# Slots of a batch ordered by key half, then head pair, with three key halves and one set of value chunks on chip, in a paged attention kernel

## The chip, the cores and the metric

One core of one Trainium2 chip. The time is the device time of one launch in microseconds; the profile is one further execution of the same program with the hardware profiler on.

## What is computed

64 sequences of 32 tokens, 512 features. First each sequence is mixed over its own tokens with one of 16 weight matrices, and added to itself:

```python
x = x + jnp.einsum('bct,bcd->bdt', x, weights[condition])     # 32 x 32 each
```

Then a layer of attention with a paged cache is added. 32 query heads share 8 key heads of 128; q and k are normed and rotated; every sequence sees up to 474 of 512 cached keys (16 pages of 32, found by a block table) and its own 32 new ones:

```python
q = rope(rmsnorm(x @ Wq.T));  k = rope(rmsnorm(x @ Wk.T));  v = x @ Wv.T
kc = k_cache[block_table].reshape(bsz, 512, 8, 128);  vc = v_cache[block_table]...
valid_c = arange(512)[None, :] < cache_seqlens[:, None]
scores = jnp.where(valid, q . concat([kc, k]) * SCALE, -1e30)
o = softmax(scores) . concat([vc, v]);   x = x + o @ Wo.T
```

## The kernel before, in words

All is fp32. The work is cut into 32 **steps**: two halves of the heads (16 query heads, 4 key heads each), and in each 16 token tiles of 128 rows. A tile is 4 sequences, called **batches** (`bt`). A step has 16 **slots**, four for each batch; a slot is numbered `g` inside its batch and `slot` inside the step. The loop over steps, batches and slots (in the part behind L1380 of the listing) calls the pieces below in the order that is written there, and the scheduler is told to keep that order on every engine, so the program order is the order of each engine's queue.

A slot deals with two of the four key heads (a pair: heads 0 and 1, or 2 and 3) against half of the 512 cached keys (256, two chunks of 128). `part_of(j)` names pair and half of slot `j`: before the change, pair 0 half 0, pair 0 half 1, pair 2 half 0, pair 2 half 1. In a slot there are:

- `scores` (L859): four products (eight rows of the profile, two passes each) of keys by queries into the PSUM tile `ps`, then `exp` on ScalarE (L870) into `pr`, of which there are two buffers. No maximum is subtracted.
- `head_keys` (L850): DVE copies the keys of the slot four ahead from `k_t` into `kh` (four buffers).
- `load_half` (issues at L324): SyncE (SP) loads half a batch of keys, eight pages, for the batch two ahead, into `k_t` (four halves). It is called at `g` = 0 and 1.
- `next_values`: ScalarE fills one chunk of `v_ring` (L370) from `raw`, multiplying by `valid`, which is 1 for keys that the sequence has and 0 for others. `v_ring` holds two batches of four chunks, each with a further column that holds `valid` itself, written on GpSimd (L373, `mask_ones`), so that the product with values also gives the sum of the softmax. Behind each fill GpSimd issues the indirect fetch of the chunk three further on (L357) into the freed `raw` (three buffers).
- `values` (L922) of the slot before: four products of `pr` by `v_ring` into the PSUM tile `po` (two buffers), which collects both halves of a pair. In the first four slots of a step they stand early in the slot, in the others at its end. After the second half of a pair, DVE adds `nv` (what the new keys gave), takes the reciprocal and multiplies (L933 to L936): "the triple".

Beside this, a step carries pieces of the steps around it: `new_scores` at slot 0 and `new_values` at slots 1 and 2 (L880, L904, with copies of `nv` on ScalarE, L912) for the new keys; `turn` (L946) of finished outputs on DVE at slots 0, 10 and 13; the output projection `out_proj` (L787) of the step before; and a `plan` of pieces that project later tiles to q, k and v. Two tiles are projected together with seven half-sized products in place of eight (L691, PSUM banks `pa`, `pb`, `pc`, sums in `u`, `z` on DVE, L707). The projections are squared on ScalarE (L474), turned into a power on GpSimd (L482, L483), rotated and scaled on DVE (L491 to L509), transposed into `rows` (L534), written to DRAM by GpSimd (L538, `heads_d`) and read back in column order by SP (L546, `spread`) into `q_ring`. `pp` names four PSUM banks that these pieces share.

Before the loop an opening, written out by hand, computes the first tiles (L1060 to L1180).

At the end of the program the softmax's sums are looked at (`in_range`); if one were out of range, the whole would run again in an exact form (`run(True)`).

Of the kernel before, what the change touches and what calls it, by code (L numbers as in the profile page):

```python
# [12 lines left out]
F32 = mybir.dt.float32  # L13
# [7 lines left out]
P = 128  # L21
# [39 lines left out]
def cond_resid_paged_attention_kernel(  # L61
# [55 lines left out]
    part = const.tile([P, 1], F32, tag="part", name="part")  # L117
    nc.vector.tensor_copy(part, part_i)

    valid = const.tile([P, B, VC], F32, tag="valid", name="valid")  # L120
# [46 lines left out]
    def cached_rows(pages_at, lens_at):  # L167

        row2 = const.tile([P, 1], F32, tag="row2", name="row2")
        nc.vector.tensor_scalar(row2, row, float(NHH), None, ALU.mult)  # L170
        nc.vector.tensor_scalar(
            v_row, pages_at, float(PSIZE * NHH), row2, ALU.mult, ALU.add
        )
        nc.vector.tensor_copy(lens_all, lens_at)
        for c in range(VC):
            key = const.tile([P, 1], F32, tag=f"key{c}", name=f"key{c}")
            nc.vector.tensor_scalar_add(key, part, float(c * P))
            nc.vector.tensor_scalar(valid[:, :, c], lens_all, key, None, ALU.is_gt)

    def other_half(by):  # L180

# [21 lines left out]
    def steps_of(exact, pools):  # L203
# [15 lines left out]
        else:  # L219
# [5 lines left out]


        v_ring = wpool.tile(
            [P, 2 * VC, GH, D + 1], F32, tag="v_ring", name=f"v_ring_{uid}"
        )

        def v_of(b):
            return v_ring[:, b % 2 * VC : (b % 2 + 1) * VC]

        vn_bufs = [
            wpool.tile([P, GH, D + 1], F32, tag=f"vn{i}", name=f"vn{i}_{uid}")
# [79 lines left out]
        def load_k(hh, b, half):  # L315

            if half == 0:
                pages_of[hh, b] = page_numbers(b)
            page = pages_of[hh, b]
            k_raw = kv.tile(  # L320
                [P, HP, GH, PSIZE], F32, tag="k_t", name=f"k_t_{hh}_{b}_{half}_{uid}", bufs=4
            )
            for j in range(HP):
                nc.sync.dma_start(  # L324
                    k_raw[:, j, :, :].rearrange("p g r -> p (g r)"),
                    kt[hh, bass.ds(page[half * HP + j], 1)].rearrange("o d e -> (o d) e"),
                )
            return k_raw

        def load_all(hh, b):  # L330
            k_raw = kv.tile([P, NPP, GH, PSIZE], F32, tag="k_all", name=f"k_t_{hh}_{b}_{uid}")
            page = page_numbers(b)
            for j in range(NPP):
                nc.sync.dma_start(
                    k_raw[:, j, :, :].rearrange("p g r -> p (g r)"),
                    kt[hh, bass.ds(page[j], 1)].rearrange("o d e -> (o d) e"),
                )
                r, c = j % BT * PSIZE, j // BT
                ins = nc.sync.dma_start(
                    v_of(b)[r : r + PSIZE, c, :, 0:D],  # L340
                    vc.rearrange("(p r h) (g d) -> p h r g d", r=PSIZE, h=NHH, g=GH)[
                        bass.ds(page[j], 1), hh
                    ].rearrange("o r g d -> (o r) g d"),
                )
                last_k[:] = [ins.ins]
            return k_raw
# [17 lines left out]
            )  # L364
            raws[n, c] = raw

        def mask_v(b, c, raw):

            ok = valid[:, b, c : c + 1]
            nc.scalar.activation(v_of(b)[:, c, :, 0:D], raw, AF.Copy, scale=ok)  # L370

        def mask_ones(b):
            nc.gpsimd.tensor_copy(  # L373
                v_of(b)[:, :, :, D], valid[:, b, :].unsqueeze(2).to_broadcast([P, VC, GH])
            )


        class Step:
# [433 lines left out]
        class Batch:  # L812


            def __init__(self, st, bt):
                self.st, self.bt = st, bt
                self.n = st.n * BT + bt
                self.name = f"{st.name}_{bt}"
                self.b = st.t * BT + bt
                self.k_raw, self.k, self.pr = [], {}, {}  # L820
                if exact:
                    self.k_raw = load_all(st.hh, self.b)
                self.v_t = v_of(self.b)

            def load_half(self):
                self.k_raw.append(load_k(self.st.hh, self.b, len(self.k_raw)))

            def fill(self, c):
                mask_v(self.b, c, raws.pop((self.n, c)))
                if c == 0:  # L830
                    mask_ones(self.b)

        def part_of(j):
            return j // 2 * 2, j % 2

        def queries(ba, g):
            return columns(ba.st, ba.bt)[:, g, :]
# [14 lines left out]

        def scores(ba, j):

            g, _ = part_of(j)
            ps = ps_s.tile([P, 2, 2, P], F32, tag="ps", name=f"ps_{ba.name}_{j}")
            for c in range(2):
                for i in range(2):
                    nc.tensor.matmul(  # L859
                        ps[:, c, i, :],  # L860
                        ba.k[j][:, i, c, :],
                        queries(ba, g + i),
                        start=True,
                        stop=True,
                    )
# [4 lines left out]
            nc.scalar.activation(pr, ps, AF.Exp, scale=SCALE)  # L870
            ba.pr[j] = pr

        def new_scores(st):
# [40 lines left out]
        def values(ba, j):  # L914


            g, half = part_of(j)
            if half == 0:
                ba.po = ps_o.tile([P, 2, D + 1], F32, tag="po", name=f"po_{ba.name}_{j}")
            for c in range(2):  # L920
                for i in range(2):
                    nc.tensor.matmul(  # L922
                        ba.po[:, i, :],
                        ba.pr[j][:, c, i, :],
                        ba.v_t[:, 2 * half + c, g + i, :],
                        start=(half == 0 and c == 0 and i == 0),
                        stop=(half == 1 and c == 1),
                        skip_group_check=True,
                    )
            if half:  # L930
                both = slice(g, g + 2)
                t = ba.st.nv[:, ba.bt, both, :]
                nc.vector.tensor_tensor(t, ba.po, t, ALU.add)  # L933
# [131 lines left out]
        spare["kh", 0, GH - 1], spare["pr", 0, 2] = early[:, 0:512], early[:, 512:1024]  # L1065
# [25 lines left out]
        load_w("q", 0, 3)  # L1091
        later = Batch(first, 1)
        later.load_half()
        later.load_half()
# [7 lines left out]
        rot_tables(first)  # L1102
        nc.vector.memset(vn_bufs[0][:, :, D : D + 1], 1.0)
        nc.vector.memset(vn_bufs[1][:, :, D : D + 1], 1.0)
        cached_rows(pages_at, lens_at)
        trig = work.tile([P, 3, TRIG * HD], F32, tag="w1", name="trig1", bufs=1)
        reduced(TRIG, trig)
# [12 lines left out]
        fetch(0, RAW, tag="pn", bufs=1)  # L1120
        q_b(first, 0)
        head_keys(batch, 0, nc.scalar)
        head_keys(batch, 1, nc.scalar)
        q_a(first, 2)
        k_b(first)
        head_keys(batch, 2, nc.scalar)
# [4 lines left out]
        after.load_half()  # L1131
        after.load_half()
        new = v_product(first)
        q_b(first, 1)
# [6 lines left out]
        batch.fill(2)  # L1141
        fetch(1, 2)
        batch.fill(3)
        scores(batch, 1)
        values(batch, 0)
        q_a(first, 3)
        q_b(first, 2)
# [1 line left out]
        keep_x1(second, nc.gpsimd)  # L1149
        head_keys(later, 0, nc.scalar)  # L1150
        head_keys(later, 1, nc.scalar)
        rot_tables(second)
        k_a(second)
        q_b(first, 3)
        scores(batch, 2)
        scores(batch, 3)
        new_scores(first)
        scores(later, 0)
        new_values(first, 0)
        values(batch, 1)  # L1160
        values(batch, 2)
        new_values(first, 2)
        for c in range(VC):
            later.fill(c)
            fetch(1 + (c + RAW) // VC, (c + RAW) % VC)
        head_keys(later, 2)
# [152 lines left out]
        valued, turned = (batch, GH - 1), [batch]  # L1319
        new_ot(first)  # L1320
        batches = {0: batch, 1: later, 2: after}
        unfilled = [(n, c) for n in range(2, NHH * NT * BT) for c in range(VC)]

        def batch_of(n):
            if n not in batches:
# [34 lines left out]
        for st in steps:  # L1360
            for bt in range(0 if st.n else 1, BT):
# [3 lines left out]
                for g in range(GH):  # L1365
# [3 lines left out]
                    while copied <= min(this.n * GH + g + KH, NHH * NT * BT * GH - 1):  # L1369
                        head_keys(batches[copied // GH], copied % GH)  # L1370
                        copied += 1
                    if g < 2 and this.n + 2 < NHH * NT * BT:
                        batch_of(this.n + 2).load_half()
                    if slot in norm_slots[min(st.n, 4 + st.n % 2)]:
                        norm_next()
# [125 lines left out]
```

## Time and profile before

| what | value |
|---|---|
| median of 3 runs | 2113.44 us (2112.53 to 2113.55) |
| the profiled execution | 2118.78 us |
| its span | 2116.8 us |
| mean granted TensorE clock | 0.994 |
| PE busy | 2082.0 us, 98% |
| DVE, ScalarE, GpSimd busy | 67%, 45%, 48% |
| DMA | 413.22 MB, 195 GB/s |

A page of the profile lists busy times by engine (PE is TensorE's matmuls, PEld its weight loads, DVE VectorE, ACT ScalarE, POOL GpSimd, SP SyncE), and then groups of instructions: the line, the engine, what is written and read, the number, busy microseconds and mean nanoseconds of one, and last how long the engine was idle just before them and what ended that. "A <- B" in a wait means that A waited for B. PEclk is the clock that TensorE was granted, 1.00 being full speed. The profiled execution is 5.3 us longer than the median of the runs; about 2 us of it lie outside the span.

### The profile page before, as it was taken

How to read it: one execution, taken by the hardware profiler on the slowest of the kernel's cores; microseconds unless marked ns; L12 is line 12 of the kernel's file. 1: busy time of each engine (PE TensorE's matmuls, PEld its weight loads, DVE VectorE, ACT ScalarE, POOL GpSimd, SP SyncE). 2: the span in 40 equal slices, each digit the busy share in tenths (PEclk: the TensorE clock that was granted, in tenths of full speed). 3: DMA queues.
4: the chain of work that ended last, by engine and by line, in shares of the span. 5: the costliest groups of instructions: out<-in, count | busy, mean ns of one | idle time of the engine just before them, and what ended most of it. 6: DMA issues, size and time to landing. Idle time of an engine off the chain costs nothing.

```text
span 2116.8 us, 43551 instructions
## 1 busy us (share of the span) xinstructions
PE 2082.0 (98%) x12804; PEld 1469.1 (69%) x12804; DVE 1423.9 (67%) x2930; ACT 960.3 (45%) x2706; POOL 1019.1 (48%) x1250
## 2 busy tenths in 40 slices
PE   7999999999999999999999999999999999999998
PEld 4766666776677766777676677767777776777775
DVE  4555676867768677686866768677676866758532
ACT  3544344544544544444444445434444444445442
POOL 4444365554636456363554535445363554535431
PEclk9999999999999999999999999999999999999999
DMA  8776547576676766787667876666766666675662
GB/s 247 196 204 203 163 133 227 165 212 185 195 215 180 215 183 189 216 253 227 198 204 208 235 213 175 206 183 186 205 192 197 179 198 182 199 205 171 194 202 69
DMA packets 410247, 413.22 MB, mean 195 GB/s; under 512 B 58928, under 2 KB 325552, under 8 KB 410000
## 3 DMA queue, kind: packets, MB, share of 16 engines
q1 hardware_dynamic: 354096, 229.87, 38.3%
q0 software_dynamic: 55168, 180.27, 28.5%
q8 instruction: 104, 1.70, 0.3%
q14 instruction: 143, 1.17, 0.2%
q10 hardware_dynamic: 736, 0.21, 0.0%
HBM read 350.09 MB, written 60.03 MB: 194 GB/s over the span
## 4 chain that ended last, share of the span: by engine, by line
PE 88%; DMA 3%; DVE 2%; SPq 2%; issue 1%; POOL 1%; ACT 1%; ACTq 0%; DVEq 0%; POOLq 0%
PE po_x L922 20%; PE pout_x L787 20%; PE ps_x L859 20%; PE pb_x L691 9%; PE pa_x L691 6%; PE pc_x L691 6%; PE pnv_x L904 2%; PE pp_q_x L465 2%; DMA k_t_x<-in_kt_dram 1%; PE psn_x L880 1%; SPq L324 1%; DMA wo_x<-in_wo_dram 1%; DMA freq<-in_inv_freq_dram 1%; POOL raw_x L357 1%; PE pp_k_x L465 0%
## 5 line engine op out<-in xcount | busy, mean ns | idle before, releaser
L357 POOL DMA_INDIRECT raw_x<-in_vc_dram,v_row x512 | 553.8, 1082 | 497.5 <-ACT v_ring_x L370 403.0
L870 ACT ACTIVATE pr_x<-ps_x 128x512 f32<-128x512 f32 x511 | 305.8, 598 | 736.1 <-PE ps_x L859 729.6
L922 PEld LDWEIGHTS po_x<-v_ring_x,pr_x 128*128 128x128 f32 x4088 | 523.5, 192 | 165.2 <-issue 147.0
L922 PE MATMUL po_x<-v_ring_x,pr_x 128*128 128x129 f32 x4088 | 548.0, 277 | 1.0 <-ACT pr_x L870 1.0
L859 PE MATMUL ps_x<-q_ring_x,kh_x 128*128 128x128 f32 x4088 | 544.7, 276 | 1.6 <-ACT q_ring_x L605 1.6
L859 PEld LDWEIGHTS ps_x<-q_ring_x,kh_x 128*128 128x128 f32 x4088 | 500.0, 192 | 21.4 <-issue 15.7
L787 PE MATMUL pout_x<-wo_x,ot_x 128*128 128x512 f32 x1024 | 477.7, 593 | 0.0
L370 ACT ACTIVATE v_ring_x<-raw_x,valid 128x512 f32<-128x512 f32 x512 | 368.9, 721 | 42.2 <-DMA raw_x<-in_vc_dram,v_row 41.8
L850 DVE COPY kh_x<-k_t_x 128x512 f32<-128x512 f32 x506 | 222.8, 442 | 221.9 <-PE ps_x L859 163.0
L538 POOL DMA_DIRECT2D heads_d<-rows_x x150 | 130.2, 868 | 444.8 <-DVE rows_x L534 412.6
L787 PEld LDWEIGHTS pout_x<-wo_x,ot_x 128*128 128x128 f32 x1024 | 189.2, 191 | 210.0 <-issue 210.0
L691 PE MATMUL pb_x<-t_x,early 128*128 128x512 f32 x504 | 239.1, 597 | 3.2 <-DVE u_x L707 2.1
L933 DVE TENSOR_TENSOR nv_x<-po_x,nv_x 128x258 f32<-128x258 f32 x256 | 106.4, 416 | 170.7 <-PE po_x L922 166.5
L483 POOL TENSOR_TENSOR rs_q_x<-ms_q_x,minus_half 128x4 f32<-128x4 f32 x128 | 137.5, 1074 | 10.7
L509 DVE TENSOR_TENSOR rope_q_x<-rope_q_x,rs_q_x 128x512 f32<-128x512 f32 x120 | 82.6, 688 | 88.8 <-POOL rs_q_x L483 88.5
L691 PEld LDWEIGHTS pb_x<-t_x,early 128*128 128x128 f32 x504 | 86.7, 192 | 65.6 <-issue 61.3
L936 DVE TENSOR_TENSOR nv_x<-nv_x,rden 128x256 f32<-128x256 f32 x256 | 112.4, 439 | 8.7
L691 PE MATMUL pa_x<-wq_x,early 128*128 128x512 f32 x224 | 105.7, 594 | 0.0
L691 PE MATMUL pc_x<-wq_x,early 128*128 128x512 f32 x224 | 105.4, 593 | 0.0
L474 ACT ACTIVATE sq_q_x<-u_x 128x128 f32<-128x128 f32 x224 | 66.3, 297 | 79.1 <-DVE u_x L707 77.9
L912 ACT COPY nv_x<-pnv_x 128x258 f32<-128x258 f32 x256 | 77.6, 396 | 46.5 <-DVE ot_x L946 31.0
L505 DVE TENSOR_TENSOR rope_q_x<-rope_q_x,ropeu_q_x 128x512 f32<-128x512 f32 x128 | 88.6, 692 | 4.4
(182 smaller groups left out, 2007.7 us busy)
## 6 DMA issues: line engine op xcount, KB each, us to landing
k_t_x<-in_kt_dram SPq DMA_DIRECT2D x2048, 64.0 KB
heads_d<-rows_x POOLq DMA_DIRECT2D x150, 256.0 KB
q_ring_x<-heads_d SPq DMA_DIRECT2D x480, 80.0 KB
raw_x<-in_vc_dram,v_row POOLq DMA_INDIRECT x512
wo_x<-in_wo_dram SPq DMA_DIRECT2D x32, 256.0 KB
res_x<-acc_d SPq DMA_DIRECT2D x31, 256.0 KB
acc_x<-in_x_dram SPq DMA_DIRECT2D x16, 256.0 KB
wq_x<-in_wq_dram SPq DMA_DIRECT2D x8, 512.0 KB
```

Source lines behind the costliest of these rows:

```text
L357: nc.gpsimd.indirect_dma_start(out=raw.rearrange("p g d -> p (g d)"), out_offset=None, in_=vc, in_offset=bass.IndirectOffsetOnAxis(ap=v_ro ...
L370: nc.scalar.activation(v_of(b)[:, c, :, 0:D], raw, AF.Copy, scale=ok)
L483: nc.gpsimd.tensor_tensor(rs, ms, minus_half, ALU.pow)
L538: nc.gpsimd.dma_start(heads_d[st.n][:, :, i, :].rearrange("k p c -> p k c"), part)
L691: nc.tensor.matmul(bank, pair.x[:, i, c, :], by[:, c * 512 : (c + 1) * 512], start=start and c == 0, stop=c == 1, skip_group_check=not start,)
L787: nc.tensor.matmul(st.po, st.ot[:, i, :], wt["o", st.hh, i // 4][:, i % 4, :], start=(i == 0), stop=(i == QH - 1),)
L850: nc.vector.tensor_copy(to, src)
L859: nc.tensor.matmul(ps[:, c, i, :], ba.k[j][:, i, c, :], queries(ba, g + i), start=True, stop=True,)
L870: nc.scalar.activation(pr, ps, AF.Exp, scale=SCALE)
L922: nc.tensor.matmul(ba.po[:, i, :], ba.pr[j][:, c, i, :], ba.v_t[:, 2 * half + c, g + i, :], start=(half == 0 and c == 0 and i == 0), stop= ...
L933: nc.vector.tensor_tensor(t, ba.po, t, ALU.add)
L936: nc.vector.tensor_tensor(t[:, :, 0:D], t[:, :, 0:D], rd.unsqueeze(2).to_broadcast([P, 2, D]), ALU.mult,)
```

## The change

The slots of a batch are taken half by half: half 0 of pair 0, half 0 of pair 2, half 1 of pair 0, half 1 of pair 2. With this:

- both `po` tiles of a batch are open at once (`po` becomes a table by pair), and the triples stand behind the values of slots 2 and 3 in place of 1 and 3;
- `v_ring` holds four chunks, not eight. In the slots with odd `g` two chunks are filled: at `g` = 1 chunks 2 and 3 of this batch, at `g` = 3 chunks 0 and 1 of the next. Each fill is still followed by the fetch three chunks further on;
- a fill is a plain copy. Absent keys get a bias of -1e30 inside the exponential (`hidden`, in place of `valid`). The bias is one value for each partition, that is for each key of one chunk, so an exponential becomes two, one for each chunk;
- the ones column is set once, by one memset; the 128 copies on GpSimd go;
- `k_t` has three halves, and `load_half` is called at `g` = 0 and 2;
- in the opening the key copies, scores and values follow the new order, the loads of second halves come later, and the second batch has only chunks 0 and 1 filled.

```diff
-            [P, 2 * VC, GH, D + 1], F32, tag="v_ring", name=f"v_ring_{uid}"
+            [P, VC, GH, D + 1], F32, tag="v_ring", name=f"v_ring_{uid}"
...
-                [P, HP, GH, PSIZE], F32, tag="k_t", name=f"k_t_{hh}_{b}_{half}_{uid}", bufs=4
+                [P, HP, GH, PSIZE], F32, tag="k_t", name=f"k_t_{hh}_{b}_{half}_{uid}", bufs=3
...
-            nc.vector.tensor_scalar(valid[:, :, c], lens_all, key, None, ALU.is_gt)
+            nc.vector.tensor_scalar(hidden[:, :, c], lens_all, key, NEG, ALU.is_le, ALU.mult)
...
-        def mask_v(b, c, raw):
-
-            ok = valid[:, b, c : c + 1]
-            nc.scalar.activation(v_of(b)[:, c, :, 0:D], raw, AF.Copy, scale=ok)
-
-        def mask_ones(b):
-            nc.gpsimd.tensor_copy(
-                v_of(b)[:, :, :, D], valid[:, b, :].unsqueeze(2).to_broadcast([P, VC, GH])
-            )
+        def fill_v(c, raw):
+
+            nc.scalar.copy(v_ring[:, c, :, 0:D], raw)
...
         def part_of(j):
-            return j // 2 * 2, j % 2
+            return j % 2 * 2, j // 2
...
-            nc.scalar.activation(pr, ps, AF.Exp, scale=SCALE)
+            for c in range(2):
+                nc.scalar.activation(
+                    pr[:, c],
+                    ps[:, c],
+                    AF.Exp,
+                    bias=hidden[:, ba.b, 2 * half + c : 2 * half + c + 1],
+                    scale=SCALE,
+                )
...
             if half == 0:
-                ba.po = ps_o.tile([P, 2, D + 1], F32, tag="po", name=f"po_{ba.name}_{j}")
+                ba.po[g] = ps_o.tile([P, 2, D + 1], F32, tag="po", name=f"po_{ba.name}_{j}")
...
+        nc.vector.memset(v_ring[:, :, :, D : D + 1], 1.0)
...
-        unfilled = [(n, c) for n in range(2, NHH * NT * BT) for c in range(VC)]
+        unfilled = [divmod(m, VC) for m in range(VC + 2, NHH * NT * BT * VC)]
...
-                    if g < 2 and this.n + 2 < NHH * NT * BT:
+                    if g % 2 == 0 and this.n + 2 < NHH * NT * BT:
                         batch_of(this.n + 2).load_half()
...
-                    if unfilled and unfilled[0] <= ((this.n + 1, g - 1) if g else (this.n, VC)):
-                        next_values()
+                    if g % 2:
+                        for _ in unfilled[:2]:
+                            next_values()
                     if slot >= GH and valued is not None:
                         values(*valued)
```

More of the change, by code (lines that the diff above doesn't have):

```diff
@@ L118, in cond_resid_paged_attention_kernel @@
     nc.vector.tensor_copy(part, part_i)
-    valid = const.tile([P, B, VC], F32, tag="valid", name="valid")
+    hidden = const.tile([P, B, VC], F32, tag="hidden", name="hidden")
     v_row = const.tile([P, B * VC], I32, tag="v_row", name="v_row")
@@ L227, in steps_of @@
         v_ring = wpool.tile(
-            [P, 2 * VC, GH, D + 1], F32, tag="v_ring", name=f"v_ring_{uid}"
+            [P, VC, GH, D + 1], F32, tag="v_ring", name=f"v_ring_{uid}"
         )
-        def v_of(b):
-            return v_ring[:, b % 2 * VC : (b % 2 + 1) * VC]
         vn_bufs = [
@@ L339, in load_all @@
                 ins = nc.sync.dma_start(
-                    v_of(b)[r : r + PSIZE, c, :, 0:D],
+                    v_ring[r : r + PSIZE, c, :, 0:D],
                     vc.rearrange("(p r h) (g d) -> p h r g d", r=PSIZE, h=NHH, g=GH)[
@@ L819, in __init__ @@
                 self.b = st.t * BT + bt
-                self.k_raw, self.k, self.pr = [], {}, {}
+                self.k_raw, self.k, self.pr, self.po = [], {}, {}, {}
                 if exact:
                     self.k_raw = load_all(st.hh, self.b)
-                self.v_t = v_of(self.b)
+                self.v_t = v_ring
             def load_half(self):
@@ L828, in fill @@
             def fill(self, c):
-                mask_v(self.b, c, raws.pop((self.n, c)))
-                if c == 0:
-                    mask_ones(self.b)
+                fill_v(c, raws.pop((self.n, c)))
         def part_of(j):
-            return j // 2 * 2, j % 2
+            return j % 2 * 2, j // 2
         def queries(ba, g):
@@ L853, in scores @@
         def scores(ba, j):
-            g, _ = part_of(j)
+            g, half = part_of(j)
             ps = ps_s.tile([P, 2, 2, P], F32, tag="ps", name=f"ps_{ba.name}_{j}")
@@ L922, in values @@
                     nc.tensor.matmul(
-                        ba.po[:, i, :],
+                        ba.po[g][:, i, :],
                         ba.pr[j][:, c, i, :],
@@ L932, in values @@
                 t = ba.st.nv[:, ba.bt, both, :]
-                nc.vector.tensor_tensor(t, ba.po, t, ALU.add)
+                nc.vector.tensor_tensor(t, ba.po[g], t, ALU.add)
                 rd = rden[:, ba.b, both]
@@ L1064, in steps_of @@
         early = work.tile([P, 7 * 2 * P], F32, tag="x", name="early", bufs=1)
-        spare["kh", 0, GH - 1], spare["pr", 0, 2] = early[:, 0:512], early[:, 512:1024]
+        spare["kh", 0, GH - 1], spare["pr", 0, 1] = early[:, 0:512], early[:, 512:1024]
         spare["trig", TRIG] = early[:, 1024:1280].rearrange("p (a t f) -> p a t f", a=2, t=TRIG)
@@ L1093, in steps_of @@
         later.load_half()
-        later.load_half()
         positions()
@@ L1122, in steps_of @@
         head_keys(batch, 0, nc.scalar)
-        head_keys(batch, 1, nc.scalar)
+        head_keys(batch, 2, nc.scalar)
         q_a(first, 2)
         k_b(first)
-        head_keys(batch, 2, nc.scalar)
+        head_keys(batch, 1, nc.scalar)
+        later.load_half()
         head_keys(batch, 3, nc.scalar)
@@ L1130, in steps_of @@
         after = Batch(first, 2)
-        after.load_half()
         after.load_half()
@@ L1143, in steps_of @@
         batch.fill(3)
-        scores(batch, 1)
+        scores(batch, 2)
         values(batch, 0)
@@ L1151, in steps_of @@
         head_keys(later, 1, nc.scalar)
+        after.load_half()
         rot_tables(second)
@@ L1154, in steps_of @@
         q_b(first, 3)
-        scores(batch, 2)
+        scores(batch, 1)
         scores(batch, 3)
@@ L1159, in steps_of @@
         new_values(first, 0)
+        values(batch, 2)
         values(batch, 1)
-        values(batch, 2)
         new_values(first, 2)
-        for c in range(VC):
+        for c in (0, 1):
             later.fill(c)
```

## The prediction

> **What bounds the kernel now.** I read the page first (busy shares, chain, groups), then a table of stretches, then the order of time around one boundary between token tiles, and the table of waits.
>
> ```profile
> span 2116.8 us, 43551 instructions
> PE 2082.0 (98%) x12804; PEld 1469.1 (69%) x12804; DVE 1423.9 (67%) x2930; ACT 960.3 (45%) x2706; POOL 1019.1 (48%) x1250
> ...
> L357 POOL DMA_INDIRECT raw_x<-in_vc_dram,v_row x512 | 553.8, 1082 | 497.5 <-ACT v_ring_x L370 403.0
> L870 ACT ACTIVATE pr_x<-ps_x 128x512 f32<-128x512 f32 x511 | 305.8, 598 | 736.1 <-PE ps_x L859 729.6
> ...
> L370 ACT ACTIVATE v_ring_x<-raw_x,valid 128x512 f32<-128x512 f32 x512 | 368.9, 721 | 42.2 <-DMA raw_x<-in_vc_dram,v_row 41.8
> ```
>
> TensorE is busy for 98% of the span and carries 88% of the chain that ended last. ScalarE, which the change touches most, is idle for half of it, and its exponentials spend 736 us waiting for scores that PE has yet to make. So only two things can move the time: PE's own work, and the few places where PE waits. The stretches say where these are:
>
> ```profile
> core 0: us, PE busy (x) PEld busy (x) DVE busy (x) ACT busy (x) POOL busy (x), PEclk, DMA share, GB/s
> 0.00:30.00 30.00, 20.55 (x64) 12.41 (x65) 12.24 (x51) 7.24 (x26) 9.74 (x23) 0.89 0.73 231
> ...
> 120.00:330.00 210.00, 202.51 (x1079) 134.00 (x1078) 140.84 (x289) 90.04 (x277) 104.78 (x137) 0.98 0.62 178
> 330.00:2040.00 1710.00, 1708.26 (x10675) 1212.09 (x10675) 1199.95 (x2426) 792.32 (x2218) 849.66 (x1014) 1.00 0.69 200
> 2040.00:2061.00 21.00, 17.31 (x153) 15.28 (x152) 6.80 (x18) 9.43 (x20) 5.97 (x8) 0.84 0.66 197
> ```
>
> From 330 to 2040 us PE idles 1.7 us of 1710, so there is nothing to win there and much to lose. From 120 to 330 us it idles 7.5, and around 2053 us there is one stall of 3.7. The opening's 9.5 (waiting for the first tile) is not touched.
>
> **PE's own work.** The change leaves the count and shapes of the matmuls alone: 4088 rows of scores and of values. A values group waits separately for the second exponential; in this trace a matmul with a wait that is already met starts after the same 110 to 112 ns as one without. Two PSUM tiles of values are now open at once, so a bank is reused two slots after its last write begins, not three. The shortest slots are 1.79 us; two of them less 1.06 of matmuls leave 2.5 us for the three DVE instructions (0.42 + 0.17 + 0.42). I take 0 for both, with 0 to +5 us for the bank.
>
> **ScalarE.** A fill loses its scale operand, an exponential becomes two halves with a bias operand. Nearest rows: the activation of 128x128 with a bias operand (L159) took 402 ns and without (L157) 310. So an operand costs 0.09, and with 598 ns for 512 columns a column costs 0.75 ns: a half takes 0.41 + 0.09 = 0.50, and two, which overlap by the 0.1 that fills in a row show, 0.90 in place of 0.60. That is 512 x 0.30 = +154 us of ScalarE; 512 fills at 0.60 instead of 0.72 give back 62. ScalarE goes from 45% to about 50%. In nearly all slots this is hidden: values start 4 to 8 us after their exponential ended. What it costs where that cover is thin comes below.
>
> **GpSimd.** 128 copies of the ones column vanish (33.5 us, 261 ns each). What I take to matter is its order: fetches now come in pairs after the fills of slots 1 and 3 of a batch, so none stands in slot 0 between the write of the last heads (L538) and the norm's power (L483).
>
> **Gains, with their place.** At 261 us DVE waits 2.45 for the power (L509), the turn of the outputs is late by that, and the chain turn, nv copies (L912), first product of the new values (L904) stalls PE 2.35 at 265.2 and 1.16 at 273.2; the clock is then 0.5 from 267.2 to 270.6, a further 1.7. A fetch of 1.08 less ahead of the power, and the DVE triple of the pair one slot later, start the turn about 1 us earlier: 2.35 becomes about 1.3, the second stall goes. Taken: -3.5 (0 to -5.2). At 321.8 PE waits 2.06 for u (L707) behind such a triple, and 1.7 goes to half clock; the triple now follows u: -2 (0 to -3.7). Stalls of 1.1 at the start of step 4 and of 0.9 and 0.25 in steps 17 and 11: -1.5 (0 to -2.2). Sum -7 (0 to -11).
>
> Here the Trainium skill ("TensorE: Matmul & The Clock Gate", Part 1) says otherwise on the clock: half rate comes after an idle window of about 3.4 us, which is free-running. By that rule none of these 2 us stalls should cost any clock, and a stall cut to 1 us would save 1 us only; by the trace (PEclk 0.79 from 266 to 274 us, 0.66 around 2053) a stall of 2 us does bring half clock for 3.4 us. The rule would make the gains -4, the rows -7. I take the rows.
>
> **Losses.** The place to look at is the boundary into an odd step, 13 times from step 5 on, where values of slot 2 start 0.6 us after their exponential. Step 7 (S0 = 537.1):
>
> ```profile
> 539.73 0.71 ACT L370 ACTIVATE v_ring_x<-raw_x,valid 128x512 f32<-128x512 f32 x1
> ...
> 541.51 0.88 POOL L538 DMA_DIRECT2D heads_d<-rows_x  x1 [1.77 <-DVE rows_x L534]
> ...
> 542.68 1.05 POOL L357 DMA_INDIRECT raw_x<-in_vc_dram,v_row  x1 [0.30 <-issue]
> ...
> 543.35 1.21 ACT L912 COPY nv_x<-pnv_x 128x258 f32<-128x258 f32 x4 [1.26 <-DVE ot_x L946]
> ...
> 544.41 0.76 ACT L370 ACTIVATE v_ring_x<-raw_x,valid 128x512 f32<-128x512 f32 x1
> ...
> 545.04 0.62 ACT L870 ACTIVATE pr_x<-ps_x 128x512 f32<-128x512 f32 x1
> ...
> 546.16 0.97 PEld L922 LDWEIGHTS po_x<-v_ring_x,pr_x 128*128 128x128 f32 x8
> ```
>
> Read it from below: values at 546.2 need the exponential that ended at 545.66, which stood behind the fill at 544.4, which stood behind the nv copies. After the change two fills stand there, the second with data fetched only after the first fill of slot 15, that is, behind the heads write at 541.5 (0.65 earlier if DVE no longer waits for the power). So: fetch at about 540.9 to 541.9, and at these boundaries a fetch landed 3.9 us after its issue (75% by 4.4, 90% by 4.8): 544.8 to 545.8. Fills 544.4 to 545.0 and, at the latest landing, 545.8 to 546.4; first half of the exponential ready at 546.9, 0.7 late; at the earliest landing 545.0 to 545.6, first half at 546.1, in time. I take 0.25 each: 13 x 0.25 = +3.3, with 0 and 13 x 1.5 = 20 as ends (beyond 2 us a stall would also bring the half clock).
>
> Here too a page speaks: "DMA: Bandwidth & Descriptors" (Anatomy of one DMA, software path) gives 2.0 us plus bytes over 436 GB/s, 2.6 us for the 256 KB of a fetch. By it the data would be there at 544.5 at the latest and this loss would be nothing. The trace has 4.3 as median over all fetches and up to 10.5, with 195 GB/s of other traffic, so the row decides.
>
> The last steps have four slots of 1.79 in a row: an odd chunk's fetch now leads its fill by two slots (3.6 us) against a landing of 4.3: +0.5 (0 to 2). The last turn of two heads now follows the values of slot 15: +0.6 (0.6 to 1). Keys: three halves in place of four shorten SP's run-ahead from six slots to five, while each half is needed later. SP needs some 4.2 us of issues per half and is waited for 28 times already (DVE kh on k_t, 51.5 us, longest 7.7); that longest one, at 2050.6, makes the stall of 3.7 at 2053.3. I take 0 there (-3 to +6). Opening, with half a load later and its fills reordered: 0 (-1 to +1). Sum +4.4.
>
> **Sum.** -7 + 4.4 = -2.6 against the profiled execution's 2118.78, so 2116.2; the median of the runs lies 5.3 lower (2113.44), so about 2111.
>
> **Rivals.**
> (1) Slower: the second fill of slot 1 comes late at every boundary. ScalarE runs in order, so the exponential of slot 2 waits behind it, and PE behind that, 1 to 1.5 us at 13 odd boundaries, and by the same path at some even ones (slack there 1.2 to 1.7). It decides when the fetch lands later than 545.2 in the picture above, 8.1 us after the step's first score. For it: the slack is 0.6, POOL waits 403 us for fills already and the lead is shorter by a slot. Against: the GpSimd order loses a fetch there. 13 to 20 us on top, less half of the gains: 2113 + 16 - 3 = about 2126. Chance 0.29.
> (2) Faster: gains as above or larger, and no loss at the boundaries: -7 to -9, about 2106. Chance 0.26. Against: all of it hangs on five places of 1 to 4 us.
> (3) Keys starve: the three halves let SP fall behind at the q_ring spreads (SP waits 150 us for scores there), DVE's copy of keys holds up what stands behind it, and PE stalls 0.5 to 1 us in many steps: 32 x 0.4 = +13, about 2124. Chance 0.06.
> (4) ScalarE becomes the bound: no, 50% busy; the split would have to cost 1 us a slot.
> (5) The change does not do what it says: absent keys give zero either way, so the exact path is not entered; 0.01.
>
> **How the numbers follow.** A run of this kernel tells about 0.2% from no change: 2109.2 to 2117.7. The balanced case (0.38) gives 2111, its own range 2106 to 2117. Faster comes from (2), and 0.06 of the balanced case; slower from (1) and (3), and little else. The 80% range leaves out the far ends of (1) and (2): 2104 to 2127.
>
> **What would show it.** Right: PE's idle time between 120 and 330 us falls from 7.5 to 3 or 4; exponential halves of 0.5 us; L509 no longer waits for L483 at boundaries; values of slot 2 in odd steps start at most 0.5 us later after the first score. Wrong: groups of values idle behind pr or v_ring in steady steps, waits of ACT for raw that grow from 41.8 us to hundreds, PEclk below 1.00 between 330 and 2040 us, or DVE waits on k_t above 100 us.

## The result, and the profile after

The changed kernel took 2140.76 us (median of 4 runs, 2132.82 to 2141.24) against 2113.49 us before: the ratio is 1.0121, with a 95% interval of 1.0097 to 1.0144. It is 27 us slower; 2111 was forecast, with 2127 as the upper end of the range. The page of the changed kernel, busy times and the groups that the change touches:

```profile
span 2139.4 us, 43815 instructions
PE 2087.2 (98%) x12804; PEld 1470.2 (69%) x12804; DVE 1415.8 (66%) x2931; ACT 1032.1 (48%) x3218; POOL 968.7 (45%) x1122
...
L354 POOL DMA_INDIRECT raw_x<-in_vc_dram,v_row x512 | 551.0, 1076 | 572.0 <-ACT v_ring_x L366 457.5
L860 ACT ACTIVATE pr_x<-ps_x,hidden 128x256 f32<-128x256 f32 x1022 | 429.6, 474 | 660.7 <-PE ps_x L848 584.3
...
L366 ACT COPY v_ring_x<-raw_x 128x512 f32<-128x512 f32 x512 | 299.0, 626 | 103.5 <-DMA raw_x<-in_vc_dram,v_row 101.5
```

ScalarE's bill came as priced: an exponential half takes 0.47 us, a fill 0.63, and the engine is 48% busy, nowhere near a bound. But fills now wait 101.5 us for their data, where they waited 41.8. The stretches show where TensorE loses:

```profile
core 0: us, PE busy (x) PEld busy (x) DVE busy (x) ACT busy (x) POOL busy (x), PEclk, DMA share, GB/s
120.00:330.00 210.00, 201.91 (x1093) 133.80 (x1092) 141.72 (x291) 97.84 (x326) 100.44 (x127) 1.00 0.59 170
330.00:2040.00 1710.00, 1691.84 (x10503) 1196.54 (x10502) 1182.14 (x2402) 840.72 (x2624) 797.04 (x897) 1.00 0.67 197
```

In the steady part, from 330 to 2040 us, PE idles 18.2 us of 1710 where it idled 1.7 (the gaps between neighbouring matmuls add up to 17.9 there). The span grew by 22.6 us. Counted by step, each from the first product of the new scores to the next one (steps are numbered from 0), the 22.6 lie in steps 1 to 3 (+5.3), in the odd steps from 5 to 29 (+8.5), in the even steps from 6 to 30 (+11.1) and in the last step (-2.2); the rest is -0.2.

What did TensorE wait for? Its own groups say it (busy, mean, idle before and what ended it):

```profile
L918 PE MATMUL po_x<-v_ring_x,pr_x 128*128 128x129 f32 x4088 | 548.1, 277 | 8.5 <-DVE nv_x L929 3.9 <-ACT v_ring_x L366 2.5 <-ACT pr_x L860 2.0
...
L900 PE MATMUL pnv_x<-vn_x,pn_x 32*128 32x129 f32 x1024 | 52.4, 298 | 9.6 <-ACT pn_x L884 6.6 <-ACT nv_x L908 1.8 <-issue 1.1
L876 PE MATMUL psn_x<-q_ring_x 128*32 128x128 f32 x1024 | 35.3, 276 | 1.3 <-DMA q_ring_x<-heads_d 1.3
L394 PE MATMUL pmix_x<-acc_x,bd 128*128 128x512 f32 x32 | 18.1, 656 | 4.4 <-DMA acc_x<-in_x_dram 4.4
...
L402 PE MATMUL px1t_x<-ident,acc_x 128*128 128x128 f32 x64 | 9.6, 275 | 3.9 <-DVE acc_x L395 3.9
```

There are three families. The values wait for fills and exponentials (2.5 and 2.0 us, mostly behind the boundary into an odd step). The product of the new values waits for `pn`, the exponential of the new scores (mostly behind the boundary into an even step). And an x tile and query columns that SP loads come late (L394, L876). Beside these, 3.9 us of the first row are the wait for a value bank that DVE still reads (`po`); the wait at L402 was 3.6 us in the kernel before and is not new.

### The profile page after: what moved, and what is told of

The parts are those of the page before. It is cut to its first block, busy times and chain, and to the rows that moved or that the text cites. A ratio compares the mean times of both kernels' runs of the same rounds, so it can differ in the third digit from the quotient of the medians.

```text
span 2139.4 us, 43815 instructions
## 1 busy us (share of the span) xinstructions
PE 2087.2 (98%) x12804; PEld 1470.2 (69%) x12804; DVE 1415.8 (66%) x2931; ACT 1032.1 (48%) x3218; POOL 968.7 (45%) x1122
## 4 chain that ended last, share of the span: by engine, by line
PE 85%; DMA 4%; DVE 3%; SPq 3%; issue 2%; ACT 2%; POOL 1%; ACTq 0%; DVEq 0%; POOLq 0%
PE pout_x L778 19%; PE po_x L918 19%; PE ps_x L848 18%; PE pb_x L682 9%; PE pa_x L682 6%; PE pc_x L682 6%; PE pnv_x L900 2%; SPq L321 2%; PE pp_q_x L456 2%; DMA k_t_x<-in_kt_dram 2%; PE psn_x L876 1%; DMA raw_x<-in_vc_dram,v_row 1%; PE pmix_x L394 1%; DMA freq<-in_inv_freq_dram 1%; POOL rs_q_x L474 1%
## 5 line engine op out<-in xcount | busy, mean ns | idle before, releaser
L860 ACT ACTIVATE pr_x<-ps_x,hidden 128x256 f32<-128x256 f32 x1022 | 429.6, 474 | 660.7 <-PE ps_x L848 584.3
L839 DVE COPY kh_x<-k_t_x 128x512 f32<-128x512 f32 x506 | 218.2, 434 | 299.5 <-PE ps_x L848 155.1
L366 ACT COPY v_ring_x<-raw_x 128x512 f32<-128x512 f32 x512 | 299.0, 626 | 103.5 <-DMA raw_x<-in_vc_dram,v_row 101.5
L474 POOL TENSOR_TENSOR rs_q_x<-ms_q_x,minus_half 128x4 f32<-128x4 f32 x128 | 146.5, 1145 | 10.7
L500 DVE TENSOR_TENSOR rope_q_x<-rope_q_x,rs_q_x 128x512 f32<-128x512 f32 x120 | 82.4, 687 | 66.5 <-POOL rs_q_x L474 64.8
```

The source lines that it names most:

```text
L366: nc.scalar.copy(v_ring[:, c, :, 0:D], raw)
L474: nc.gpsimd.tensor_tensor(rs, ms, minus_half, ALU.pow)
L839: nc.vector.tensor_copy(to, src)
L860: nc.scalar.activation(pr[:, c], ps[:, c], AF.Exp, bias=hidden[:, ba.b, 2 * half + c : 2 * half + c + 1], scale=SCALE,)
```

## Why SP is late

SP's waits, of the kernel before (in all, times, longest):

```profile
SPq L546 <- PE ps_x L859: 150.4, 28, 11.2
SPq L324 <- DVE nv_x L933: 77.6, 16, 8.0
...
SPq L324 <- DVE kh_x L850: 39.6, 34, 8.6
```

and of the changed kernel:

```profile
SPq L321 <- DVE kh_x L839: 244.5, 87, 10.1
SPq L537 <- PE ps_x L848: 41.8, 19, 3.9
SPq L321 <- DVE nv_x L929: 25.0, 9, 3.7
```

The rows that name `nv` are waits for key copies too: in nearly all of their time SP's load starts within 0.1 us of the end of a copy of keys, and the DVE instruction behind the copy is named in its place. So SP stood about 117 us at key loads before, until DVE had copied the last keys out of a half, and 150 us at the query columns (L546), waiting for scores to free their place. In the changed kernel it is 270 us at the key loads and 42 at the query columns. SP takes its instructions in the order in which they are written, so all that stands behind a key load waits too. Here is such a place, the x tile that TensorE needs late in step 3. SP waited for key copies until 313.6 us (10.1 us long) and again until 321.6 (2.8), and issued the loads that stood there before it came to these:

```profile
327.09 4.52 SPq L537 DMA_DIRECT2D q_ring_x<-heads_d  x5
...
331.71 0.84 SPq L382 DMA_DIRECT2D acc_x<-in_x_dram  x2
...
335.63 2.08 PE L394 MATMUL pmix_x<-acc_x,bd 128*128 128x512 f32 x2 [4.40 <-DMA acc_x<-in_x_dram]
```

The tile was issued at 331.7 and wanted at 331.2 (before: issued at 325.3, wanted at 332.4). TensorE stood 4.40 us, and the granted clock was 0.5 from 333.3 to 340.1. The stalls in this step that the change was forecast to shorten did shrink in sum: 2.06 at 321.8 became 0.80, and 2.35 and 1.16 became 1.61, 0.32 and 0.75, none of them with half clock. The stall for the tile took this back; step 3 is 1.9 us longer than before.

## The experiments

All ratios are to the kernel before on the same chip; its median was 2113.5 to 2118.0 us on the chips used.

**The parts of the change.** First the masking alone, on the kernel before:

```diff
-            nc.scalar.activation(v_of(b)[:, c, :, 0:D], raw, AF.Copy, scale=ok)
+            nc.scalar.copy(v_of(b)[:, c, :, 0:D], raw)
...
-            nc.scalar.activation(pr, ps, AF.Exp, scale=SCALE)
+            for c in range(2):
+                nc.scalar.activation(
+                    pr[:, c],
+                    ps[:, c],
+                    AF.Exp,
+                    bias=hidden[:, ba.b, 2 * half + c : 2 * half + c + 1],
+                    scale=SCALE,
+                )
```

> The kernel before with only the masking changed: bias in the exponential (two halves), plain fills, ones column set once; slot order, eight value chunks, one fill a slot and four key halves stay. Theory F (the fills in pairs, with data fetched late, hold up ScalarE's queue): about 2112 to 2115, no stall at the boundaries. Rival S (the split exponential lengthens ScalarE's queue at the even boundaries, so that the exponential of the new scores comes 0.6 late): 2119 to 2125, PE waiting for pn at even boundaries.

Measured 2113.9 us, ratio 0.9993 (0.9981 to 1.0005). The bias, the split and the 128 copies less on GpSimd, taken together, cost nothing and bring nothing that these runs show.

Then the order alone: the changed kernel with the old masking, eight chunks, four halves.

> The changed kernel with the old masking, eight value chunks, one fill a slot a batch ahead and four key halves: what is left is the order of the slots, both value banks open, and the key loads at g = 0 and 2. Theory F: 2109 to 2115. Rival O (the order itself, through the banks or the triples, costs the time): 2125 or more.

2116.1 us, ratio 1.0001 (0.9993 to 1.0010). The order alone is free as well. TensorE now waits for a value bank (5.7 us for DVE's triple in this trace), but the wait of the new values for their copies, 6.0 us before, is down to 0.6.

> New slot order and new masking together, but eight value chunks filled one a slot a batch ahead, and four key halves: all of the change but what it saves on chip. If the loss comes from the small ring and the three halves: 2110 to 2117, as each of the two alone. If order and masking harm only together: 2125 or more.

2116.7 us, ratio 1.0004 (0.9996 to 1.0011). Both together are free. So all of the loss belongs to what the change saves on chip: four value chunks in place of eight, with the fills in pairs that go with them, and three key halves in place of four.

**Four halves, and fills one a slot.** Two single edits of the changed kernel:

```diff
-name=f"k_t_{hh}_{b}_{half}_{uid}", bufs=3
+name=f"k_t_{hh}_{b}_{half}_{uid}", bufs=4
```

> The changed kernel with four key halves in place of three. Theory F: only the 4.4 us stall for the x tile at 335.6 us and a few small ones go, 2134 to 2140. Rival K (SP's shorter run-ahead on keys costs most of the time): 2120 or less.

2136.2 us, ratio 1.0111 (1.0092 to 1.0130): the stall for the x tile was gone, but the time is within what was said for the theory that the fills were most of it.

```diff
-                    if g % 2:
-                        for _ in unfilled[:2]:
-                            next_values()
+                    while unfilled and unfilled[0] <= divmod(this.n * VC + g + 1, VC):
+                        next_values()
```

> The changed kernel with one fill a slot (chunk 1 of a batch at g = 0, 2 at 1, 3 at 2, 0 of the next at 3), all else as changed. Theory F: 2116 to 2125, since each fetch leads its fill by three slots again and only one fill stands before an exponential. Rivals S and K: 2136 to 2141, as the change.

2168.8 us, ratio 1.026 (1.0231 to 1.0290). This contradicts the theory: filling in pairs is better than this alternative. With one fill a slot a chunk is filled one slot before its use. Was it that its data came late? The same with five buffers for fetched chunks (`LEAD = 5` in place of `RAW`, with two more fetches in the opening) answers that:

> One fill a slot with the small ring (which took 2169) and five buffers for fetched chunks. Theory L: its loss was data that landed after its fill was due, with the fill one slot before its use, so 2120 to 2132 here. If the loss is that a fill stands before its values by one slot only, however early the data is: 2145 or more.

2161.0 us, ratio 1.0214 (1.0190 to 1.0238): the rival is right. Its trace has no row of fills that wait for data, and still

```profile
L919 PE MATMUL po_x<-v_ring_x,pr_x 128*128 128x129 f32 x4088 | 558.2, 278 | 28.1 <-ACT v_ring_x L367 22.1 <-DVE nv_x L930 6.0
```

TensorE waits 22 us for the fill itself, 0.45 to 0.8 us in every step from 4 to 30 (once 1.8): a fill that stands behind an exponential, one slot ahead of the values, is too late here in a slot of 1.79 us, however early its data is.

**Five buffers for fetched chunks, pairs kept.** The expectations from here on speak of held or late semaphores. A semaphore is a counter by which one engine tells another that it is done. In the trace of the change, and in those of the masking, the order, the four halves and the one fill a slot, such a signal at times takes effect late: an engine starts up to 2 us after what it waited for has ended, though it is free. The traces of some chips do not show this. The first run has five buffers and fetches in pairs, the second five buffers and one fetch a slot.

> The changed kernel with five buffers for fetched chunks in place of three, so that a fetch leads its fill by four slots or more; fills and fetches stay in pairs. Theory L (data that lands late is most of the loss): the stalls of values at about 945, 993 and 1204 us go, 2125 to 2132. Theory H (two fetches issued back to back hold the semaphores of the other engines, so that the exponential of the new scores comes 2 us late): the waits for pn at the starts of even steps stay at 0.4 to 0.8 each, about 8 us in all, so no better than 2125. If neither: 2140.

2127.4 us, ratio 1.0063 (1.0046 to 1.0080).

> As the run with five buffers, but with one fetch issued in each slot in place of two in every second slot; the fills stay in pairs. Theory H: the exponential of the new scores starts within 0.7 us of their end, and PE's waits for it at even steps vanish: 7 to 9 us less than with pairs, 2116 to 2124. Theory L alone: the same time as with pairs, within 2 us.

2125.0 us, ratio 1.0051 (1.0035 to 1.0068). In both traces the waits of values for fills are gone; what is left stands mostly at SP's loads (3.2 us each at L395 and L877 with pairs, 3.0 and 3.3 with one fetch a slot). But the waits for `pn` were gone with pairs too, which neither theory had said. So the kernel before was traced on this chip:

> The kernel before, unchanged, for a trace of the same day as the others. In the traces of the changed kernel and of the runs so far, the semaphore updates of TensorE, VectorE and ScalarE that fall into the last third of a fetch's issue by GpSimd come only some 0.5 us after that issue ended; in the first trace of the kernel before they came at once. If the hold belongs to the chip, it is here too: the exponential of the new scores starts 0.3 to 0.6 us after they ended at the starts of even steps, not 0.07, and the span is within 0.3% of 2116.8. If it belongs to the changed kernels, it is not here.

There are none here: the exponential of the new scores started 0.04 to 0.07 us after their end in every step, and the span was 2114.3. None of the traces of this chip shows late semaphores. Later runs say that it is not the kernel: the version with five buffers and pairs shows them on another chip, and the change does not show them on a third. They come with the chip, or with how its trace is taken.

**The change and both remedies on one chip.** This chip shows the late semaphores again.

> The changed kernel, unchanged, beside the next three on one chip. Theory L (late data and the short lead of the fetches make most of the loss): 2133 to 2142 on any chip, with values waiting for fills at the starts of odd steps. If the held semaphores were the cause, and this chip does not hold them, it is below 2126.

2139.2 us, ratio 1.0107 (1.0089 to 1.0124).

> The changed kernel with five buffers for fetched chunks and four key halves; small ring, fills and fetches in pairs. With five buffers alone it took 2127, and what was left stood in steps 2, 3 and 31, where TensorE waited for an x tile and for the query columns behind SP's key loads. Theory L with K for the rest: 2114 to 2120. If the three halves cost nothing: 2125 to 2129.

2126.4 us, ratio 1.0044 (1.0028 to 1.0061): 12.8 us less than the change, but 6 above what was expected. In its trace TensorE waits 7.0 us for `pn`, about that much; that this wait is the whole difference is not shown.

> Five buffers, four key halves, fills in pairs but one fetch a slot. Theory L with K: 2114 to 2119, as with the fetches in pairs (difference under 3); on a chip that holds the semaphores during a fetch's issue, 4 to 8 less than with pairs.

2127.5 us, ratio 1.0051 (1.0034 to 1.0069), no better than in pairs. The trace shows why it could not be: in the short slots 14, 15 and 0 two fetches that stand in neighbouring slots are still issued back to back (in step 10 at 0.23 to 1.17 and 1.48 to 2.42 us from the step's start).

The wait for `pn` can be read in one trace, that of the change on this chip (of the slowest of its four executions, 2147.3 us). The start of step 10:

```profile
737.29 1.08 PE L876 MATMUL psn_x<-q_ring_x 128*32 128x128 f32 x32
737.54 0.95 POOL L354 DMA_INDIRECT raw_x<-in_vc_dram,v_row  x1 [2.36 <-ACT v_ring_x L366]
737.69 0.85 ACT L860 ACTIVATE pr_x<-ps_x,hidden 128x256 f32<-128x256 f32 x2
...
738.80 0.95 POOL L354 DMA_INDIRECT raw_x<-in_vc_dram,v_row  x1 [0.30 <-issue]
739.30 1.06 PE L848 MATMUL ps_x<-q_ring_x,kh_x 128*128 128x128 f32 x8
740.48 0.60 ACT L884 ACTIVATE pn_x<-psn_x 128x512 f32<-128x512 f32 x1 [1.94 <-PE ps_x L848]
...
741.13 0.73 PE L900 MATMUL pnv_x<-vn_x,pn_x 32*128 32x129 f32 x16 [0.77 <-ACT pn_x L884]
```

The new scores (L876) end at 738.37, ScalarE is free at 738.54, and yet their exponential starts at 740.48, once the second fetch has been issued. In step 8 of the same trace the second fetch comes later:

```profile
607.65 1.08 PE L876 MATMUL psn_x<-q_ring_x 128*32 128x128 f32 x32
607.90 0.94 POOL L354 DMA_INDIRECT raw_x<-in_vc_dram,v_row  x1 [2.35 <-ACT v_ring_x L366]
...
609.43 0.60 ACT L884 ACTIVATE pn_x<-psn_x 128x512 f32<-128x512 f32 x1 [0.44 <-PE psn_x L876]
...
610.01 0.94 POOL L354 DMA_INDIRECT raw_x<-in_vc_dram,v_row  x1 [1.17 <-issue]
610.64 0.73 PE L900 MATMUL pnv_x<-vn_x,pn_x 32*128 32x129 f32 x16
```

The exponential starts 0.70 us after the scores' end (608.73), 0.59 after the end of the one fetch, and TensorE does not wait.

**Halves on one chip, and the change without late semaphores.**

```diff
+                    if (st.n % 2, slot) not in ((1, 15), (0, 0)):
+                        for _ in unfetched[: 1 + (len(unfetched) > 2)]:
+                            fetch(*unfetched.pop(0))
```

> Five fetch buffers, four key halves, one fetch a slot, and none in slot 15 of an odd step nor in slot 0 of the even step after it; they follow in later slots. Theory H (two fetches back to back hold the semaphore updates): no wait for pn at the starts of even steps, 2115 to 2120 where the same without the gap took 2127. If the waits have another cause: 2125 to 2129.

2119.9 us, ratio 1.0019 (1.0008 to 1.0030). It says nothing on the fetches: this chip's traces show no late semaphores, and the trace has two fetches back to back at the same place as without the gap, since GpSimd reaches the earlier ones only then. But it comes closest to the kernel before of all versions with the small ring.

> The same with three key halves. Theory K (the third half is missed in steps 2, 3 and 31): 3 to 7 above the run with four, so 2119 to 2126. If the halves don't matter: within 2.

2134.8 us, ratio 1.0083 (1.0064 to 1.0101): with three halves 15 us more than with four, twice what was expected. Its trace:

```profile
L877 PE MATMUL psn_x<-q_ring_x 128*32 128x128 f32 x1024 | 36.6, 279 | 5.8 <-DMA q_ring_x<-heads_d 5.0 <-DMA k_t_x<-in_kt_dram 0.8
L395 PE MATMUL pmix_x<-acc_x,bd 128*128 128x512 f32 x32 | 17.9, 642 | 4.0 <-DMA acc_x<-in_x_dram 4.0
```

In the run with four halves these two rows have 0.0 and 1.0 us of idle time. By step the difference is 5.8 us in step 3, with stalls of 2.75 and 1.23 us for the tile, and 7.0 in step 31, with one of 4.27 for query columns; in each, 6.8 us at half clock stand beside them. SP waits 254 us for key copies with three halves and 70 with four.

> The change itself on this chip: 2136 to 2142 with held semaphores, 2128 to 2134 if this chip doesn't hold them.

2134.5 us, ratio 1.0093 (1.0076 to 1.0110), at the upper edge of what was said for a chip without late semaphores. The group of the new values in its trace:

```profile
L900 PE MATMUL pnv_x<-vn_x,pn_x 32*128 32x129 f32 x1024 | 50.2, 297 | 2.6 <-ACT nv_x L908 1.6 <-ACT pn_x L884 1.0
```

Against 9.6 us in the first trace of the same kernel. The time is 5 to 6 us lower too, but the chips' own differences (before: 2113.5 to 2118.0) are of that size and the intervals of the ratios overlap. By step it is clearer: the even steps from 6 to 30 grew by 5.4 us here, by 11.1 and 13.4 in the change's two traces with late signals.

**The two remedies side by side**, on a chip with late semaphores.

> The change with four key halves, three fetch buffers. If the two causes add up: about half of the loss of 20 to 25 us, 2124 to 2130. If four halves help only together with the buffers: 2132 or more.

2136.3 us, ratio 1.0094 (1.0073 to 1.0114).

> The change with three key halves, five fetch buffers. Adding up: 2124 to 2130. If SP's queue alone decides: 2132 or more.

2136.1 us, ratio 1.0099 (1.0078 to 1.0119).

> Both: 2117 to 2121 on a chip whose traces show no held semaphores, 2124 to 2128 on one that holds them, and in either case below each of the other two by 4 us or more if they add up.

2127.5 us, ratio 1.0050 (1.0031 to 1.0068). In time, neither alone gets clear of the change (2134 to 2141 on other chips; it was not run on this one); together they do, and with five buffers three halves cost 8.6 us here. On a chip without late semaphores, five buffers alone gave 2127.4. In the traces each remedy does its own part. Four halves alone:

```profile
L918 PE MATMUL po_x<-v_ring_x,pr_x 128*128 128x129 f32 x4088 | 548.9, 277 | 10.7 <-ACT pr_x L860 7.8 <-DVE nv_x L929 2.7
...
L394 PE MATMUL pmix_x<-acc_x,bd 128*128 128x512 f32 x32 | 16.7, 604 | 0.3 <-DMA acc_x<-in_x_dram 0.2
```

Five buffers alone:

```profile
L919 PE MATMUL po_x<-v_ring_x,pr_x 128*128 128x129 f32 x4088 | 548.2, 277 | 3.0 <-DVE nv_x L930 2.8 <-issue 0.2
...
L395 PE MATMUL pmix_x<-acc_x,bd 128*128 128x512 f32 x32 | 18.2, 658 | 3.7 <-DMA acc_x<-in_x_dram 3.7
```

Both:

```profile
L919 PE MATMUL po_x<-v_ring_x,pr_x 128*128 128x129 f32 x4088 | 546.3, 276 | 3.0 <-DVE nv_x L930 2.8 <-issue 0.2
L901 PE MATMUL pnv_x<-vn_x,pn_x 32*128 32x129 f32 x1024 | 50.5, 297 | 9.3 <-ACT pn_x L885 8.0 <-ACT nv_x L909 1.3
...
L395 PE MATMUL pmix_x<-acc_x,bd 128*128 128x512 f32 x32 | 16.2, 593 | 0.0
```

With both, the waits for fills and for SP's loads are gone and 12 us remain. Of its stalls that the kernel before did not have, the largest are the wait for `pn` (8.0 us), the value bank (2.8) and one of 2.45 us at 1108.8 for a sum on DVE. The count by step, each trace against the first one of the kernel before, says what each remedy does:

| trace | steps 1 to 3 | odd, 5 to 29 | even, 6 to 30 | last step |
|---|---|---|---|---|
| the change | +5.3 | +8.5 | +11.1 | -2.2 |
| four halves | +0.9 | +12.8 | +13.0 | -4.7 |
| five buffers | +5.9 | +0.4 | +8.3 | -0.5 |
| both | -0.9 | +3.0 | +7.7 | -2.0 |
| the change, no late signals | +2.2 | +6.7 | +5.4 | -1.3 |
| both and one fetch a slot with the gap, no late signals | +1.2 | +3.1 | 0.0 | -6.0 |

The last step differs by 4.3 us between two traces of the kernel before, and the order and masking with nothing saved, which cost no time, have +3.2 in the odd steps. So four halves take away the loss of steps 1 to 3, five buffers that of the odd steps, and what remains with both lies in the even steps, where it is gone on the chip without late signals. Four halves alone lose again in steps 12 and 13 (+10.7, the change +3.2) what they gain elsewhere: the values wait 7.8 us for late exponentials, and two spells of half clock stand there, at 948 behind such a wait of 3.4 us and at 931 behind one of 2.6 for a sum on DVE. Why these waits are longer than in the change's own trace is not settled. No version beats the kernel before; the one that keeps eight chunks and four halves equals it.

## Why the prediction was wrong, point by point

The sum of waits was -2.6 us, and the spans grew by 22.6. These terms of it failed: the even boundaries, which had no term, grew by 11.1; the shorter run-ahead of the keys, put at 0, brought the late x tile and query columns; the gains of step 3, put at -5.5, did not come (+1.9, and +2.8 in step 2, which had no term); and the odd boundaries, put at +3.3, grew by 8.5. The shares of the 27 us are not exact: with five buffers and four halves 8 to 12 us remain on the chips with late semaphores and 3.7 on the one without.

- **What bounds the kernel** (PE, with 1.7 us of idle time from 330 to 2040): right, and it is the reason that the change had little to win and much to lose.
- **PE's own work at 0 (0 to +5 for the bank)**: the work was right, the bank was not free. Its waits are 3.9 us of idle time in the change's trace, and 2.7 to 6.5 in all traces with the new order.
- **ScalarE at half 0.50, fill 0.60, hidden**: the sizes were right (0.47 and 0.63). They were not hidden behind the boundaries, see below.
- **GpSimd's order**: the mechanism is there; DVE's wait for the power (L509, now L500) fell from 88.5 to 64.8 us, and of the stall of 2.35 us at 265 only 0.32 is left. But a stall of 1.61 for the value bank now stands before it, and the sum of gains, -7, did not come: it counted stalls where they stood, not what comes next in the same stage. PE's idle time from 120 to 330 us, which was to fall from 7.5 to 3 or 4, is 8.1.
- **Clock**: that a stall of about 2 us brings half clock holds only at times. The stall of 2.51 us that ended at 1203.9 brought 3.4 us of it, but one of 3.21 us that ended at 201.5 in the same trace brought none. The same stall stands in ten other traces; it brought 3.4 us in seven and 6.8 in three. A stall of 1.61 at 265 brought none here and 3.4 in the change's two other traces. So it is partly luck that the shortened stalls brought none. In all twenty traces the spells of half clock begin whole multiples of 3.41 us apart (in the kernel before at 14.6, 267.2, 321.8 and 2052.3), so what a stall costs also hangs on where it falls. The rule that the prediction set against the rows, from the Trainium skill ("TensorE: Matmul & The Clock Gate", Part 1), half rate after an idle window of about 3.4 us, does not hold here either if it is taken as the length of a stall: stalls of 2.0 to 2.5 us did bring half clock. That its window is free-running fits the multiples.
- **Odd boundaries, +3.3**: the mechanism was right, the size too small. Values wait 4.5 us for fills and exponentials in the change's trace, with 3.4 us at half clock behind one of the waits; the odd steps grew by 8.5. It is not 13 times 0.25, but a few large ones:

```profile
942.06 0.65 ACT L366 COPY v_ring_x<-raw_x 128x512 f32<-128x512 f32 x1
...
944.01 0.62 ACT L366 COPY v_ring_x<-raw_x 128x512 f32<-128x512 f32 x1 [1.30 <-DMA raw_x<-in_vc_dram,v_row]
...
944.54 0.83 ACT L860 ACTIVATE pr_x<-ps_x,hidden 128x256 f32<-128x256 f32 x2
...
945.06 1.16 PE L918 MATMUL po_x<-v_ring_x,pr_x 128*128 128x129 f32 x8 [1.00 <-ACT pr_x L860]
```

  In this trace step 13 loses 1.0 us here and step 17 2.5; in the other odd steps TensorE waits at most 0.4 us at this place. The fetches behind these two were issued 4.8 and 6.3 us before their fill could start, where the prediction had 4.8 for nine in ten. The 2.6 us for a fetch that the prediction worked out from the Trainium skill ("DMA: Bandwidth & Descriptors", Anatomy of one DMA) would have left none of it.
- **"I take 0 there (-3 to +6)" for the keys**: this step failed. I costed the run-ahead (six slots to five) only by the keys' own use, and found that no key would be late. DVE did wait longer for keys (87.6 us after 51.5), but no product of scores stood for one. What was late stood behind the keys in SP's queue: an x tile and the query columns. The prediction named SP's wait at the q_ring spreads, but took it, in rival (3), for the place where SP would fall behind, when it was the sign of SP's lead: 150 us of waiting at L546 were the reserve, and 42 were left. Measured, with five fetch buffers: 15 us on one chip (2119.9 to 2134.8) and 8.6 on another (2127.5 to 2136.1). With three buffers, as in the change, four halves gained nothing clear of the noise (2136.2 and 2136.3).
- **Even boundaries**: not priced at all beyond "some even ones", and those by another path. On chips with late semaphores TensorE waits there for `pn`, 0.2 to 0.8 us in most even steps (6.6 us, and 1.8 for the copies that follow), and almost not at all on the others. That two fetches are now issued back to back was said, but as a gain for GpSimd's order. What makes the signals late stays open.
- **Rivals**: the truth lies on the side of (1) and (3), both at once, and neither was given enough; 0.35 of the chances were theirs, and the range stopped at 2127, at one of them alone.

## What to carry to other kernels

A queue that takes its work in order can fail not at the transfer whose buffer was taken away, but at what stands behind it: before taking a buffer from a stream, list what shares its queue, and ask whether a long wait of that queue at a later item is its reserve. In this kernel a ring that is filled just ahead of its use needed two of the shortest slots between fill and use, even with the data there. And where a kernel is 98% on one engine, a change that saves memory is judged by its worst boundary, so several small unknowns there should be added up rather than taken at their likeliest one by one.

## What the runs showed of the hardware

In twelve of the twenty traces about a fifth of the semaphore updates have no record (50,819 records in the change's first trace, 62,011 in the one without late signals); in the others nearly all have one. Only these twelve show late signals.

They stand beside the issue of indirect fetches, which takes 0.95 us. In the trace with steps 8 and 10 above, the exponential of the new scores starts 1.7 to 2.1 us after their end in 13 of the 15 even steps from 2 to 30, each time 0.5 to 0.8 us after the end of the second of two fetches. With one fetch it is less: in step 8 it starts 0.59 us after that fetch, and in the masking-only version, where the fetch ended 0.14 us before the new scores, 0.4 to 0.6 us after the scores in most even steps. But two fetches back to back are not enough: in the trace of the change without late signals they are issued at the same times of the step, and the exponential starts 0.07 us after the scores' end in 12 of these 15 steps. Whether this is a property of the chips, or the recording of the trace itself holds the signals, could not be told apart, since every trace that lacks records has late signals and no other has. A version that was to move the two fetches away from the even boundary did not move them.

The clock makes runs of one kernel differ too. Between 60 us and the last 40 us, the traces have 3.4 to 23.9 us at half clock, and by an estimate from this half of it is lost, so differences of a few us between single traces are in part the clock's. Of the 18.2 us between the spans of the two versions with four and three halves on one chip, 13.7 us more at half clock are worth about 7 by the same estimate.
